# Second attention layer: score tiles of 64 columns, blockwise fetches, maxima turned by a 4-byte transfer, a longer lead

## The chip, the core and the metric

The kernel runs on one core of a Trainium2 chip, as one program launch. The metric is device time in microseconds (us), the median over several executions. Beside it stands one execution taken by the hardware profiler, from which every row below comes. Engines: PE is the matrix engine, PEld its weight loads, DVE the vector engine, ACT the scalar engine, POOL GpSimd, SP the engine whose queue issues nearly all of the DMA transfers here.

## What is computed

Two layers follow one another, on `x` of 2 x 2048 tokens and 256 features, in f32. Each computes attention on a layer norm, times a gate from another network, and adds that to `x`. Only the attention of the second layer is touched. It has 16 heads of 16 features and a band: a query sees the keys at most 64 tokens away.

```python
band = jnp.abs(idx[:, None] - idx[None, :]) <= WINDOW // 2      # WINDOW = 128
...
scores = jnp.einsum('bhqd,bhkd->bhqk', q, k) * SCALE + mask
attn = jax.nn.softmax(scores, axis=-1)
out = jnp.einsum('bhqk,bhkd->bhqd', attn, v)
...
x = x + s * g
```

## The kernel before

One function, `attention`, serves both layers; `local` is true for the second. Its work is cut into 32 **items**, one for each batch row `b` (2), group `g` of four heads (4) and block `n` of 512 queries (4). In the second layer an item has two **units** of two query tiles of 128 each (`U = 2`), 64 units in all. The four heads of a group lie on the partitions 0 to 31, 32 to 63 and so on of the tiles `q` and `k`, so each head's matmul uses 32 rows of PE's array.

Each unit is worked on in two passes. The **first pass** finds each query's greatest score: `sq` is a score tile with queries on the 128 output partitions and a reach of 256 keys in the free dimension (192 at the two ends of the sequence). DVE adds the band's mask to it and takes the maximum in one instruction (`seen`, result in `mx`, L674). The **second pass** computes the scores again with keys on the partitions (`sk`), with the query's maximum already subtracted: row `HD` of each head's 32 rows of `q` carries the negative maximum, against a row of ones in `k`. ACT takes the exponential out of PSUM (L683), POOL zeroes what lies outside the band (four `affine_select` per unit, L688), and two units later PE multiplies by the values (`acc`, L747, with the softmax's sum in an extra column). ACT copies the sum out to `av` (L752).

`scores` issues the matmuls of both passes for one step. Before they are issued they are sorted by a number, `when`, so that matmuls of different heads alternate and their tiles run beside each other. The first pass runs ahead of the second: at step `s` the second pass is at unit `s`, the first at unit `s + U + LEAD`. `LEAD` is 3 in the second layer, so the first pass is five units ahead.

Maxima come to where they are needed in `place_max` (from L714): PE transposes `mx` into PSUM (`pmx`, L720), ACT copies it negated to `row` (L723), and ACT's own queue issues a transfer of `row` into `q` (L726). The first layer does it in another way, with `turn_max` and `fetch_max` (L700 to L712): DVE negates into `nmx`, SP writes it to DRAM in turned order (`md`), and three units later SP fetches it back into `q`.

Division by the softmax's sum takes a round trip through DRAM, all by SP, in program order: `av` to `ad` (L773), the sums back as `dn` and the numerators to `xn` (L782, L783), DVE's reciprocal (L786), `dn` to `rd` (L789), and `rd` spread to `recb` (L796). Then `divide` multiplies, by turns on POOL and on DVE (L802). After the last group of a block, `project` multiplies by the output weights (L835) and updates `x`.

`fetch` brings `k` and `q` of a head group from DRAM (`qd`) by SP, in halves of the sequence, into one of two pairs of tiles. The dictionary `after` names the step after which each of these helpers is called. What is wrapped in `pin` keeps its program order on its engine; the rest is ordered by the framework. SP executes its queue in order, so a transfer that waits holds up those behind it.

Of the kernel before, what the change touches and what calls it, by code (L numbers as in the profile page):

```python
# [10 lines left out]
F32 = mybir.dt.float32  # L11
I32 = mybir.dt.int32
AF = mybir.ActivationFunctionType
ALU = mybir.AluOpType
# [3 lines left out]
P = 128  # L18
# [19 lines left out]
def two_layers(ctx: ExitStack, tc: tile.TileContext, a, out):  # L38
# [445 lines left out]
    def attention(A, scale, local, final, start=None, projected=False):  # L484
# [15 lines left out]
        U = TT // 2 if local else NT  # L500
        LEAD = 3 if local else 6
        DEL = 2 if local else 1
        with ExitStack() as st:
# [44 lines left out]
            mp, op = pool("mp", 2), pool("op", 1)  # L548
            hp = [slice(j * HP, (j + 1) * HP) for j in range(NG)]
            ep = None if local else pool("ep", 8)  # L550


            pmax, pm = pool("pmax", 2, space=PSUM), pool("pexp", 4, space=PSUM)
            if local:

                mask = mp.tile([P, 2 * P], F32, name="mask", bufs=1)
                nc.vector.memset(mask, 0.0)
                nc.gpsimd.affine_select(
                    out=mask, in_=mask, compare_op=ALU.is_ge, fill=MASKED, base=0,
                    pattern=[[1, 2 * P]], channel_multiplier=-1,  # L560
                )
                nc.gpsimd.affine_select(
                    out=mask, in_=mask, compare_op=ALU.is_ge, fill=MASKED, base=P,
                    pattern=[[-1, 2 * P]], channel_multiplier=1,
                )

                efirst = xn[1].rearrange("p c t -> p (c t)").rearrange("p (i s c f) -> p i s c f", i=4, c=2, f=P)
                elast = op.tile([P, 2, 4, 2, P], F32, name="elast")
                ecount = [0]

                def exponentials():

                    r = ecount[0] % 6
                    ecount[0] += 1
                    return efirst[:, r] if r < 4 else elast[:, r - 4]
# [4 lines left out]

            def fetch(bg, lo=0, hi=T):

                if bg >= B * NG:
                    return
                b, g = divmod(bg, NG)
                k0, k1 = max(lo - PAD, 0), (T if hi == T else hi - PAD)
                for i, t in ((1, qs[bg % 2]), (0, ks[bg % 2])):
                    to, s = (slice(lo, hi), slice(lo, hi)) if i else (slice(PAD + k0, PAD + k1), slice(k0, k1))
                    nc.sync.dma_start(out=t[:, to], in_=qd[i, b, bass.ts(g, NG), :, s].rearrange("h w t -> (h w) t"))
# [6 lines left out]
            def scores(second, first, es):  # L596
# [7 lines left out]
                if second:  # L604
# [3 lines left out]
                    if local:  # L608

                        qt = n * TT + 2 * u  # L610
                        segs = [
                            (P, 3 * P, bass.ts(qt + 1, P), bass.ds(qt * P, 2 * P)),
                            (0, P, bass.ts(qt, P), bass.ts(qt, P)),
                            (3 * P, 4 * P, bass.ts(qt + 2, P), bass.ts(qt + 1, P)),
                        ]
                    else:
                        segs = [(0, TB, bass.ts(u, P), bass.ts(n, TB))]
                    if local:
# [7 lines left out]
                    for j in range(NG):  # L626
# [4 lines left out]
                        else:  # L631
                            t = pm.tile([P, TB], F32, name="sk", tag="m")
                        when = 2 * (j // 2) if apart else 0
                        for lo, hi, ks_, qs_ in segs:
                            pieces.append((when, t[:, lo:hi], k[hp[j], ks_], q[hp[j], qs_]))
                            when += 2 * (hi - lo) / TB
                        tasks.append((es[j], t))
                pairs = []
                if first:
# [9 lines left out]
                    for pair in ((2, 3), (0, 1)):  # L649
                        sq = pmax.tile([P, 2, TB], F32, name="sq", tag="sq")  # L650
                        pairs.append((pair, sq))
                        for d, j in enumerate(pair):
                            when = (2, 2, 0, 0)[j] if apart else 0
                            if local:
                                for t in range(2):
                                    qt, lo, hi = reach(n1, u1, t)
                                    pieces.append((
                                        when + t, sq[:, d, t * 2 * P + lo : t * 2 * P + hi],
                                        q1[hp[j], bass.ts(qt, P)], k1[hp[j], qt * P + lo : qt * P + hi],
                                    ))  # L660
                            else:
# [6 lines left out]
                for pair, sq in pairs:  # L668
                    if local:
                        for d, j in enumerate(pair):  # L670
                            for t in range(2):
                                qt, lo, hi = reach(n1, u1, t)
                                seen = mp.tile([P, 2 * P], F32, name="seen", tag="seen")
                                nc.vector.tensor_tensor_reduce(  # L674
                                    seen[:, lo:hi], sq[:, d, t * 2 * P + lo : t * 2 * P + hi], mask[:, lo:hi],
                                    1.0, LOWEST, ALU.add, ALU.max, mx[:, j, 2 * u1 + t : 2 * u1 + t + 1],
                                )
# [14 lines left out]

            def reach(n, u, t):

                qt = n * TT + 2 * u + t
                return qt, (PAD if qt == 0 else 0), (2 * P - PAD if qt == NT - 1 else 2 * P)

            pin = tc.keep_in_program_order
# [8 lines left out]
            def fetch_max(i):  # L707
# [3 lines left out]
                    in_=md[i % 2].rearrange("(j t) p -> j (t p)", t=TT),  # L711
                ))  # L712

            def place_max(i):  # L714

                b, g, n = items[i]
                q = tiles(i)[0]
                mx, _ = part.pop(i)
                ps = pm.tile([NG * TT, P], F32, name="pmx", tag="m")
                nc.tensor.transpose(ps, mx.rearrange("p j t -> p (j t)"), ident)  # L720
                row = mp.tile([NG * TT, P], F32, name="row", tag="row", bufs=2 if local else 1)
                if local:
                    pin(nc.scalar.activation(row, ps, AF.Copy, scale=-1.0))  # L723
                else:
                    nc.vector.tensor_scalar(row, ps, -1.0, None, ALU.mult)
                pin((nc.scalar if local else nc.sync).dma_start(  # L726
                    out=q[HD:P:HP, bass.ts(n, TB)].rearrange("j (t c) -> j t c", c=P), in_=row
                ))
# [69 lines left out]
            def divide(i):  # L798

                b, g, n = items[i]  # L800
                pin(
                    (nc.vector if local and i % 2 else nc.gpsimd).tensor_tensor(together(b, g, n), together(b, g, n), divs.pop(i), ALU.mult)  # L802
                )
# [55 lines left out]
            for i, (b, g, n) in enumerate(items):  # L859
                if local:  # L860
                    at(i * U - LEAD, place_max, i)
                else:
                    at(i * U - LEAD, turn_max, i)
                    at(i * U - LEAD + 3, fetch_max, i)
                end = (i + 1) * U
# [324 lines left out]
```

## Time and profile before

| | us |
|---|---|
| median of three runs | 2537.28 |
| their range | 2533.64 to 2539.33 |
| the profiled execution | 2538.34 |
| its span | 2536.6 |

The second layer's attention begins at 2248 us of the span and fills the rest of it. Busy time of the engines there, by stretches, from the windows view:

| stretch, us | what runs | PE | DVE | ACT | POOL |
|---|---|---|---|---|---|
| 2248 to 2303 | last projections of keys, queries and values, first pass ahead, then both begin | 53.9 | 24.3 | 25.6 | 7.9 |
| 2303 to 2405 | both passes | 101.3 | 92.8 | 75.5 | 84.9 |
| 2405 to 2453 | both passes with output projections | 47.9 | 36.9 | 25.7 | 39.7 |
| 2453 to 2496 | both passes | 41.7 | 39.0 | 31.0 | 36.4 |
| 2496 to 2537 | second pass alone, last projections | 35.6 | 19.0 | 16.7 | 24.6 |

How such rows are read: a line of a group begins with the kernel's line number and the engine, then the operation, the tile written, an arrow and the tiles read, and the shape. For PE, `32*128 32x256` is a tile of 32 rows and 128 columns of the array, through which 256 columns of moving data stream. A product of f32 matrices is two such instructions in the trace. PE counts as busy while any matmul is in flight, so a busy PE need not be at its peak.

### The profile page before, as it was taken

The numbers are of one execution on the slowest core, as the hardware profiler recorded it, in microseconds if no ns is written. First come the engines' busy times: TensorE is split into PE (matmuls) and PEld (weight loads), VectorE is DVE, ScalarE is ACT, GpSimd is POOL, SyncE is SP. The second block draws the span as 40 slices with busy tenths as digits, with TensorE's granted clock in tenths as the row PEclk, the third lists the DMA queues.
The fourth block names the chain that finished last, engine by engine and source line by source line (L and its number), as shares of the span: only waits on it lengthen the run. The fifth ranks groups of instructions, "written<-read, shape, count | busy, mean of one in ns | idle before, by whom it ended". The sixth has DMA issues, their size and how long they took to land.

```text
span 2536.6 us, 47898 instructions
## 1 busy us (share of the span) xinstructions
PE 2513.1 (99%) x18896; PEld 1060.6 (42%) x18896; DVE 1686.2 (66%) x2747; ACT 1620.8 (64%) x3187; POOL 876.6 (35%) x827
## 2 busy tenths in 40 slices
PE   8999999999999999999999999999999999999999
PEld 6444444444333333333333333333333334457766
DVE  4143333157888888888777788788888765238986
ACT  5400000126888888888888888888888886227755
POOL 0000000102444444444444444444444420016887
PEclk9999999999999999999999999999999999999999
DMA  6131111230001001001001001001000002133552
GB/s 243 50 84 51 52 51 39 82 118 14 14 14 43 16 12 44 16 12 44 16 12 43 10 18 44 12 17 43 15 14 10 14 14 63 49 133 108 163 167 81
DMA packets 146353, 129.83 MB, mean 51 GB/s; under 512 B 93456, under 2 KB 97936, under 8 KB 143568
## 3 DMA queue, kind: packets, MB, share of 16 engines
q1 hardware_dynamic: 144256, 125.46, 16.5%
q8 instruction: 148, 2.42, 0.4%
q10 hardware_dynamic: 1872, 1.31, 0.2%
q14 instruction: 77, 0.63, 0.1%
HBM read 80.50 MB, written 45.97 MB: 50 GB/s over the span
## 4 chain that ended last, share of the span: by engine, by line
PE 79%; DMA 1%; ACT 0%; POOL 0%; DVE 0%; issue 0%; ACTq 0%; SPq 0%; POOLq 0%; DVEq 0%
PE sk L667 25%; PE acc L747 22%; PE sq L667 19%; PE pp L477 5%; PE pr L835 2%; PE pp L532 2%; PE po L1027 1%; PE pt L1023 1%; PE po L1035 1%; PE xb L113 0%; PE xb L138 0%; DMA k<-qd 0%; PE of L827 0%; DMA q<-qd 0%; POOL xn L688 0%
## 5 line engine op out<-in xcount | busy, mean ns | idle before, releaser
L679 DVE TENSOR_REDUCE part<-sq 128x2 f32<-128x1024 f32 x1024 | 1207.3, 1221 | 294.3 <-PE sq L667 284.7
L683 ACT ACTIVATE e<-sk 128x512 f32<-128x512 f32 x2048 | 1058.3, 603 | 217.2 <-PE sq L667 197.7
L667 PE MATMUL sk<-q,k 32*128 32x512 f32 (+2 forms) x5632 | 1135.8, 533 | 1.2 <-ACT xn L683 1.0
L667 PE MATMUL sq<-k,q 32*128 32x512 f32 (+2 forms) x5120 | 1129.1, 569 | 0.5 <-DVE part L679 0.5
L761 POOL TENSOR_TENSOR av<-av,more 128x512 f32<-128x512 f32 x459 | 581.4, 1267 | 936.3 <-ACT more L760 931.1
L667 PEld LDWEIGHTS sk<-q,k 32*128 32x128 f32 x5632 | 522.0, 184 | 604.1 <-ACT e L683 512.5
L747 PE MATMUL acc<-e,v 128*32 128x512 f32 x4096 | 546.7, 605 | 0.0
L667 PEld LDWEIGHTS sq<-k,q 32*128 32x128 f32 x5120 | 402.3, 183 | 22.3 <-DVE part L679 13.2
L760 ACT COPY more<-acc 128x512 f32<-128x512 f32 x459 | 268.7, 585 | 1.2 <-PE acc L747 1.0
L747 PEld LDWEIGHTS acc<-e,v 128*32 128x32 f32 x4096 | 81.8, 108 | 388.2 <-ACT e L683 367.8
L461 ACT ACTIVATE gt<-po 128x512 f32<-128x512 f32 x16 | 8.8, 594 | 321.1 <-PE po L457 321.1
L674 DVE CUSTOM_DVE_ANT_0 seen<-sq,mask 128x256 f32<-128x256 f32 (+1 forms) x512 | 176.2, 410 | 53.6 <-PE sq L667 49.2
L467 POOL TENSOR_TENSOR x<-x,up 128x512 f32<-128x512 f32 x16 | 23.1, 1461 | 450.1 <-DVE up L464 277.5
L448 DVE TENSOR_TENSOR xs<-we,px 128x512 f32<-128x512 f32 x64 | 43.9, 686 | 136.2 <-PE px L440 130.3
L688 POOL TENSOR_SCALAR_AFFINE_SELECT xn<-xn 128x512 f32<-128x512 f32 x172 | 106.2, 652 | 77.4 <-ACT xn L683 75.7
L440 PE MATMUL px<-xn,FV 128*128 128x512 f32 x256 | 121.2, 595 | 0.0
L444 PE MATMUL py<-cum,FW 128*128 128x512 f32 x256 | 120.5, 593 | 0.6 <-DVE cum L412 0.6
L424 PE MATMUL po<-pr,UO 128*128 128x512 f32 x256 | 119.0, 592 | 0.0
L683 ACT ACTIVATE xn<-sk 128x512 f32<-128x512 f32 x172 | 89.8, 602 | 41.1 <-PE sk L667 17.9
L450 DVE TENSOR_TENSOR pr<-xs,py 128x512 f32<-128x512 f32 x64 | 44.0, 687 | 64.8 <-PE py L444 64.6
L424 PEld LDWEIGHTS po<-pr,UO 128*128 128x128 f32 x256 | 48.6, 190 | 61.2 <-issue 61.0
L444 PEld LDWEIGHTS py<-cum,FW 128*128 128x128 f32 x256 | 48.4, 190 | 61.5 <-issue 59.8
(195 smaller groups left out, 1604.0 us busy)
## 6 DMA issues: line engine op xcount, KB each, us to landing
we<-wd SPq DMA_DIRECT2D x128, 128.0 KB
ad<-av SPq DMA_DIRECT2D x59, 256.0 KB
qd<-sb SPq DMA_DIRECT2D x48, 256.0 KB
k<-qd SPq DMA_DIRECT2D x10, 1024.0 KB
q<-qd SPq DMA_DIRECT2D x10, 1024.0 KB
xn<-ad SPq DMA_DIRECT2D x59, 128.0 KB
recb<-rd SPq DMA_DIRECT2D x59, 128.0 KB
q<-qd SPq DMA_DIRECT2D x12, 512.0 KB
```

Source lines behind the costliest of these rows:

```text
L424: nc.tensor.matmul(po[oc], UO[:, ch, bass.ts(oc, P)], pr, start=(ch == 0), stop=False)
L440: nc.tensor.matmul(px, FV[:, c, bass.ts(ch, P)], xn[b][:, c, cols], start=(c == 0), stop=(c == NC - 1))
L444: nc.tensor.matmul(py, FW[:, c, bass.ts(ch, P)], cum[:, c, :], start=(c == 0), stop=(c == NC - 1))
L477: nc.tensor.matmul(ps, w[:, c, bass.ts(hf, P)], xn[b][:, c, bass.ts(n, TB)], start=(c == 0), stop=(c == NC - 1))
L667: nc.tensor.matmul(o, lhs, rhs, start=True, stop=True)
L674: nc.vector.tensor_tensor_reduce(seen[:, lo:hi], sq[:, d, t * 2 * P + lo : t * 2 * P + hi], mask[:, lo:hi], 1.0, LOWEST, ALU.add, ALU.max, ...
L679: nc.vector.tensor_reduce(pt[:, pair[0] : pair[1] + 1, t, kb], sq, AX.X, ALU.max)
L683: nc.scalar.activation(e, t, AF.Exp, scale=scale)
L688: nc.gpsimd.affine_select(out=e[:, :, c, :], in_=e[:, :, c, :], compare_op=ALU.is_ge, fill=0.0, base=0, pattern=[[0, 4], [sign, P]], chann ...
L747: nc.tensor.matmul(acc[hp[j], o : o + hi - lo], vs[b][:, kt, vcols(g, j)], es[j][:, lo:hi], start=(r == 0), stop=(r == len(parts) - 1), sk ...
L760: nc.scalar.copy(more, acc)
L761: nc.gpsimd.tensor_tensor(avs[i], avs[i], more, ALU.add)
```

## The change

Six edits, all to the second layer:

- First pass: a tile of 128 queries becomes two halves of 64, each with its own window of 192 keys. The two halves write partitions 0 to 63 and 64 to 127 of the same PSUM tile. The mask is built once in three forms (inside, first tile, last tile).
- Second pass: each block of 128 keys is split into two halves of 64 too, with the same moving data. The matmuls of both passes now use tiles of 32 rows and 64 columns.
- Maxima go the way of the first layer, `turn_max` and `fetch_max`; `place_max` is removed.
- The first pass runs eight units ahead (`LEAD` 6).
- `k` and `q` are fetched by blocks of 512 tokens, after every item, `k` one unit before `q`.
- `divide` goes to DVE in three of four items, not in two of four.

```diff
-        LEAD = 3 if local else 6
+        LEAD = 6
...
+            halves = [slice(sub * P // 2, (sub + 1) * P // 2) for sub in range(2)]
+            RC = P + 2 * PAD // 2
...
+                mask = mp.tile([P, 3, RC], F32, name="mask", bufs=1)
+                for m in range(3):
+                    for sub, p in enumerate(halves):
+                        nc.vector.tensor_copy(mask[p, m, :], reach[p, sub * PAD : sub * PAD + RC])
+                nc.vector.memset(mask[halves[0], 1, :PAD], MASKED)
+                nc.vector.memset(mask[halves[1], 2, RC - PAD :], MASKED)
...
-            def fetch(bg, lo=0, hi=T):
+            def fetch(bg, lo=0, hi=T, which=(1, 0)):
...
                         segs = [
-                            (P, 3 * P, bass.ts(qt + 1, P), bass.ds(qt * P, 2 * P)),
-                            (0, P, bass.ts(qt, P), bass.ts(qt, P)),
-                            (3 * P, 4 * P, bass.ts(qt + 2, P), bass.ts(qt + 1, P)),
+                            (sub, lo, hi, bass.ds((qt + kt) * P + sub * PAD, PAD), bass.ds(q0, hi - lo))
+                            for kt, lo, hi, q0 in (
+                                (1, P, 3 * P, qt * P), (0, 0, P, qt * P), (2, 3 * P, 4 * P, (qt + 1) * P)
+                            )
+                            for sub in range(2)
                         ]
...
-                        when = 2 * (j // 2) if apart else 0
-                        for lo, hi, ks_, qs_ in segs:
-                            pieces.append((when, t[:, lo:hi], k[hp[j], ks_], q[hp[j], qs_]))
-                            when += 2 * (hi - lo) / TB
+                        when = [1.5 * (j // 2) if apart and local else 2 * (j // 2) if apart else 0] * 2
+                        for sub, lo, hi, ks_, qs_ in segs:
+                            o = t[:, lo:hi] if sub is None else t[halves[sub], lo:hi]
+                            pieces.append((when[sub or 0], o, k[hp[j], ks_], q[hp[j], qs_]))
+                            when[sub or 0] += 2 * (hi - lo) / TB
...
                                 for t in range(2):
-                                    qt, lo, hi = reach(n1, u1, t)
-                                    pieces.append((
-                                        when + t, sq[:, d, t * 2 * P + lo : t * 2 * P + hi],
-                                        q1[hp[j], bass.ts(qt, P)], k1[hp[j], qt * P + lo : qt * P + hi],
-                                    ))
+                                    for sub in range(2):
+                                        q0 = (n1 * TT + 2 * u1 + t) * P + sub * PAD
+                                        pieces.append((
+                                            when + t * RC / (2 * P), sq[halves[sub], d, bass.ts(t, RC)],
+                                            q1[hp[j], bass.ds(q0, PAD)], k1[hp[j], bass.ds(q0, RC)],
+                                        ))
...
-                                seen = mp.tile([P, 2 * P], F32, name="seen", tag="seen")
+                                seen = mp.tile([P, RC], F32, name="seen", tag="seen")
                                 nc.vector.tensor_tensor_reduce(
-                                    seen[:, lo:hi], sq[:, d, t * 2 * P + lo : t * 2 * P + hi], mask[:, lo:hi],
+                                    seen, sq[:, d, bass.ts(t, RC)], mask[:, (qt == 0) + 2 * (qt == NT - 1), :],
                                     1.0, LOWEST, ALU.add, ALU.max, mx[:, j, 2 * u1 + t : 2 * u1 + t + 1],
                                 )
...
-            def place_max(i):
...
-                    (nc.vector if local and i % 2 else nc.gpsimd).tensor_tensor(together(b, g, n), together(b, g, n), divs.pop(i), ALU.mult)
+                    (nc.vector if local and i % 4 else nc.gpsimd).tensor_tensor(together(b, g, n), together(b, g, n), divs.pop(i), ALU.mult)
...
-                if local:
-                    at(i * U - LEAD, place_max, i)
-                else:
-                    at(i * U - LEAD, turn_max, i)
-                    at(i * U - LEAD + 3, fetch_max, i)
+                at(i * U - LEAD, turn_max, i)
+                at(i * U - LEAD + 3, fetch_max, i)
...
-                if local and n == NB // 2 - 1:
-                    at(end, fetch, b * NG + g + 2, 0, T // 2)
-                if n == NB - 1:
-                    at(end, fetch, b * NG + g + 2, T // 2 if local else 0)
+                if local:
+
+                    for hop, which in enumerate((0, 1)):
+                        at(end + hop, fetch, b * NG + g + 2, n * TB, (n + 1) * TB, (which,))
+                elif n == NB - 1:
+                    at(end, fetch, b * NG + g + 2)
```

More of the change, by code (lines that the diff above doesn't have):

```diff
@@ L554, in attention @@
             if local:
-                mask = mp.tile([P, 2 * P], F32, name="mask", bufs=1)
-                nc.vector.memset(mask, 0.0)
+                reach = mp.tile([P, 2 * P], F32, name="reach", bufs=1)
+                nc.vector.memset(reach, 0.0)
                 nc.gpsimd.affine_select(
-                    out=mask, in_=mask, compare_op=ALU.is_ge, fill=MASKED, base=0,
+                    out=reach, in_=reach, compare_op=ALU.is_ge, fill=MASKED, base=0,
                     pattern=[[1, 2 * P]], channel_multiplier=-1,
@@ L562, in attention @@
                 nc.gpsimd.affine_select(
-                    out=mask, in_=mask, compare_op=ALU.is_ge, fill=MASKED, base=P,
+                    out=reach, in_=reach, compare_op=ALU.is_ge, fill=MASKED, base=P,
                     pattern=[[-1, 2 * P]], channel_multiplier=1,
                 )
+                mask = mp.tile([P, 3, RC], F32, name="mask", bufs=1)
[4 more added lines that the diff above has]
+                nc.vector.memset(mask[halves[1], 2, RC - PAD :], MASKED)
                 efirst = xn[1].rearrange("p c t -> p (c t)").rearrange("p (i s c f) -> p i s c f", i=4, c=2, f=P)
@@ L586, in fetch @@
                 k0, k1 = max(lo - PAD, 0), (T if hi == T else hi - PAD)
-                for i, t in ((1, qs[bg % 2]), (0, ks[bg % 2])):
+                for i in which:
+                    t = (ks, qs)[i][bg % 2]
                     to, s = (slice(lo, hi), slice(lo, hi)) if i else (slice(PAD + k0, PAD + k1), slice(k0, k1))
@@ L611, in scores @@
                         segs = [
-                            (P, 3 * P, bass.ts(qt + 1, P), bass.ds(qt * P, 2 * P)),
-                            (0, P, bass.ts(qt, P), bass.ts(qt, P)),
-                            (3 * P, 4 * P, bass.ts(qt + 2, P), bass.ts(qt + 1, P)),
+                            (sub, lo, hi, bass.ds((qt + kt) * P + sub * PAD, PAD), bass.ds(q0, hi - lo))
[3 more added lines that the diff above has]
+                            for sub in range(2)
                         ]
                     else:
-                        segs = [(0, TB, bass.ts(u, P), bass.ts(n, TB))]
+                        segs = [(None, 0, TB, bass.ts(u, P), bass.ts(n, TB))]
                     if local:
@@ L671, in scores @@
                             for t in range(2):
-                                qt, lo, hi = reach(n1, u1, t)
-                                seen = mp.tile([P, 2 * P], F32, name="seen", tag="seen")
+                                qt = n1 * TT + 2 * u1 + t
+                                seen = mp.tile([P, RC], F32, name="seen", tag="seen")
                                 nc.vector.tensor_tensor_reduce(
-                                    seen[:, lo:hi], sq[:, d, t * 2 * P + lo : t * 2 * P + hi], mask[:, lo:hi],
+                                    seen, sq[:, d, bass.ts(t, RC)], mask[:, (qt == 0) + 2 * (qt == NT - 1), :],
                                     1.0, LOWEST, ALU.add, ALU.max, mx[:, j, 2 * u1 + t : 2 * u1 + t + 1],
@@ L691, in scores @@
                             )
-            def reach(n, u, t):
-                qt = n * TT + 2 * u + t
-                return qt, (PAD if qt == 0 else 0), (2 * P - PAD if qt == NT - 1 else 2 * P)
             pin = tc.keep_in_program_order
@@ L711, in fetch_max @@
                     in_=md[i % 2].rearrange("(j t) p -> j (t p)", t=TT),
-                ))
-            def place_max(i):
[L716 to L721, printed above, removed]
-                if local:
-                    pin(nc.scalar.activation(row, ps, AF.Copy, scale=-1.0))
-                else:
-                    nc.vector.tensor_scalar(row, ps, -1.0, None, ALU.mult)
-                pin((nc.scalar if local else nc.sync).dma_start(
-                    out=q[HD:P:HP, bass.ts(n, TB)].rearrange("j (t c) -> j t c", c=P), in_=row
                 ))
@@ L859, in attention @@
             for i, (b, g, n) in enumerate(items):
-                if local:
-                    at(i * U - LEAD, place_max, i)
-                else:
-                    at(i * U - LEAD, turn_max, i)
-                    at(i * U - LEAD + 3, fetch_max, i)
+                at(i * U - LEAD, turn_max, i)
+                at(i * U - LEAD + 3, fetch_max, i)
                 end = (i + 1) * U
```

## Prediction

> **What bounds the kernel now.** I read the page's chain first, to see whether one engine carries the end.
>
> ```profile
> PE 79%; DMA 1%; ACT 0%; POOL 0%; DVE 0%; issue 0%; ACTq 0%; SPq 0%; POOLq 0%; DVEq 0%
> ```
>
> Nearly all that is named is PE. The change touches layer two's attention alone, which fills the span from 2248 us on, so an average over the span says little. The windows view gives 102 us of its steady stretch, before any output projection:
>
> ```profile
> core 0: us, PE busy (x) PEld busy (x) DVE busy (x) ACT busy (x) POOL busy (x), PEclk, DMA share, GB/s
> 2303.00:2405.00 102.00, 101.30 (x2022) 81.21 (x2023) 92.79 (x519) 75.45 (x173) 84.92 (x132) 1.00 0.53 162
> ```
>
> DVE at 91% and POOL at 83% stand close behind PE. PE's own limit is seen in the timeline of one unit, matmuls (PE) and weight loads (PEld), start and length in us:
>
> ```profile
> 2345.19 0.48 PE L667 MATMUL sk<-q,k 32*128 32x256 f32 x2
> ...
> 2345.20 0.48 PE L667 MATMUL sq<-k,q 32*128 32x256 f32 x2
> 2345.29 0.19 PEld L667 LDWEIGHTS sk<-q,k 32*128 32x128 f32 x2
> ...
> 2345.51 0.38 PE L667 MATMUL sk<-q,k 32*128 32x256 f32 x2
> ...
> 2347.30 1.08 PE L747 MATMUL acc<-xn,v 128*32 128x128 f32 x24
> ...
> 2348.31 0.28 PE L720 MATMUL pmx<-ident,mx 128*16 128x128 f32 x1
> ...
> 2348.51 0.48 PE L667 MATMUL sk<-q,k 32*128 32x256 f32 x1
> ```
>
> Four matmuls, one per head's 32 rows, start together, and the next round follows about 0.216 us later per 256 columns (0.32 at a refill). So a unit is 2.11 us of scores, 1.01 us of acc, and in every second unit 0.20 us of pmx. The starts of acc in the trace lie 3.12 and 3.39 us apart in turn, with hardly an outlier: an item (two units) costs 6.51 us and **PE sets it**.
>
> **The change part by part, for one item.**
>
> *Half tiles on PE.* A score tile is now 32 rows by 64 columns, so eight fit. Per head and unit a tile streams 512 columns for sk and two times 192 for sq, against 512 and 512. A column costs 0.216/256 = 0.844 ns, and each product is two instructions: (512+384) x 2 x 0.844 = 1.51 us, against 1.73. The other 0.38 us of the 2.11 are two refills of 0.105 (a 128-column load takes 0.185; a 16-column load 0.088 and a 32-column one 0.109, so about 0.13 for 64), a 0.07 wait and the drain. I take 0.27. Score phase 1.78, unit 1.78 + 1.01 = 2.79. This rests on eight tiles running beside each other, which no row shows: rows show four by rows (above) and four by columns (acc). Ends: 1.51 us (all eight) and 3.02 us (two halves of a row group take turns). I take the first, because acc already runs several column tiles over the same rows.
>
> [...] the loads at 2345.29 run under the matmuls of the same heads, begun at 2345.19, and the acc group's 24 loads run under its own matmuls. By the row the loads cost nothing more, and I keep 2.79. [...]
>
> *The transpose goes.* pmx (0.20 on PE), its copy row (0.26 on ACT) and ACT's transfer issue (0.55) leave each item. PE per item: 2 x 2.79 = **5.58** instead of 6.51.
>
> *Maxima on DVE.* The edge tiles show the new form already:
>
> ```profile
> 2249.48 0.42 DVE L674 CUSTOM_DVE_ANT_0 seen<-sq,mask 128x256 f32<-128x256 f32 x1
> 2249.83 0.08 DVE L674 DVE_READ_ACCUMULATOR2_ANT mx<- 128x1 f32 x1
> 2249.83 0.35 DVE L674 CUSTOM_DVE_ANT_0 seen<-sq,mask 128x192 f32<-128x192 f32 x1
> 2250.10 0.08 DVE L674 DVE_READ_ACCUMULATOR2_ANT mx<- 128x1 f32 x1
> ```
>
> Start to start it is 0.345 for 256 columns and 0.275 for 192. Sixteen per item: 5.5 becomes 4.4. Added: nmx 0.17 (layer one's row), a quarter more of the divides (825 ns each on DVE, 0.21). With the reciprocal 0.25, DVE goes from 6.16 to **5.44**. The divide waits for recb; behind it in DVE's queue stand the next maxima, and the score matmuls wait for their PSUM.
>
> *POOL and ACT.* POOL: eight selects 4.9 plus a quarter of 1.27: 5.2 (was 5.5). ACT: eight exponentials 4.12 plus two copies 0.80: 4.9 (was 5.7). Neither is the bound.
>
> *Transfers of 4-byte elements.* Layer one does this. Its trace, an issue at 1722.89, by the microsecond:
>
> ```profile
> 1723.00:1724.00 1.00, 1.00 (x12) 0.26 (x7) 0.65 (x1) 0.75 (x2) 0.99 (x1) 1.00 0.10 1
> 1724.00:1725.00 1.00, 1.00 (x12) 0.16 (x8) 1.00 (x2) 1.00 (x3) 0.27 (x1) 1.00 0.75 7
> 1725.00:1726.00 1.00, 1.00 (x15) 0.65 (x15) 0.71 (x1) 0.80 (x2) 0.06 (x1) 1.00 0.08 1
> ```
>
> 2064 packets are through about 2.3 us after the issue began. [...] By the row it is 0.93 us of all engines' time (the three shares), 16% of a 5.8 us item atop 53% now: dear, but three units lie between write and fetch, so I cost its latency at nothing. If that cover is gone, ACT's exponentials and PE wait.
>
> *SP's queue.* This is where the change pays. Issues per item now: ad 0.54, dn 0.54, xn 0.60, rd 0.58, recb 0.53, and a k/q pair (0.82) in every second item: 3.2 us. After: the same five, a pair every item (0.82), md 0.38, q<-md 0.53: 4.52, plus nine gaps of 0.06 = 5.06 us. SP also waits in order; its waits in the 102 us (total, times, longest):
>
> ```profile
> SPq L796 <- DMA rd<-dn: 26.7, 13, 4.2
> SPq L782 <- DMA ad<-av: 9.8, 6, 4.3
> ```
>
> That is 2.05 us per recb, worst behind big fetches:
>
> ```profile
> 2357.27 0.53 SPq L589 DMA_DIRECT2D k<-qd  x1
> 2357.89 0.38 SPq L589 DMA_DIRECT2D q<-qd  x1
> 2358.32 0.58 SPq L789 DMA_DIRECT2D rd<-dn  x1
> 2358.95 1.37 SPq L773 DMA_DIRECT2D ad<-av  x1
> 2363.58 0.53 SPq L796 DMA_DIRECT2D recb<-rd  x1
> ```
>
> The fastest rd-to-recb is 1.95 us (2323.41 to 2325.36), of which rd, ad, md and their gaps will cover 1.6. So the wait is 0.3 at best and 1.5 or more behind a 256 KB pair (half the former size, but in every item). Cycle 5.4 to 6.6 or more; I take **5.95**, nearer the middle since smaller fetches spread the load. So behind PE, SP is late next.
>
> *Eight units ahead, fetch by block.* A fetched block has five or six units before its first use instead of seven; at 2.8 us that is 14 us or more against a landing of 2 to 5, hidden. Three more units run maxima alone at the start (about 0.9 us of PE each, under the last projections), three more run scores alone at the end (2.5 instead of 2.8, set by POOL and ACT). Shorter maxima in the other five give 1.2 back: +0.5 in sum, unsure by 3. The mask's six extra copies fall where DVE idles 8 us before 2249: nothing.
>
> *Sum.* Of 28 items with both passes, 20 have fetches and no projection: 20 x (6.51 - 5.95) = 11.2. Four have projections (units of 4.9 to 5.1, PE's) and four no fetch left; both follow PE's 5.58, with 0.07 for jitter: 8 x (6.51 - 5.65) = 6.9. Together 18.1, less 0.5 for the ends, less 0.2 per fetched item for divides that wait in DVE's queue (4): **about -13.5 us**. Against the profiled execution's own 2538.3 us (span 2536.6) this gives 2524.8; the three runs shown have the median 2537.3, 1.0 lower, so I say **2524**.
>
> **Rivals.**
> - *SP becomes the bound and loses* (slower). Place: recb, waiting behind rd in SP's queue, with a fetch pair ahead in every item; dn, q<-md and the DVE divide follow late. If each item pays the 2.05 us measured per recb plus a little on ad, a cycle is 7.3 us: 20 x 0.8 = +16, less 6.8 elsewhere, gives 2546. It decides from a cycle over 6.85, where 20 x 0.34 eats the 6.8 that the other items gain. For: SP has 4.5 us of issues where it had 3.2. Against: md and the fetches fill part of what was waiting, and the projections' 10 us items let SP catch up.
> - *Half tiles take turns*: score phase 3.3, unit 4.3, +1.18 x 56 = +66, 2603. For: no row shows eight. Against: both four-way rows.
> - *No full gain*: DVE, POOL and SP all within 10% of PE trade waits, an item near 6.4: 2534.
> - *Pure PE bound*: every plain item at 5.6, 24 x 0.91 + 3.4 = 25, 2512.
>
> **How the numbers follow.** 0.2%, 5.1 us here, is about what a measurement of this kernel can tell from no change. Forecast and pure PE bound together (2510 to 2532) 0.61; no full gain 0.14, mostly within 0.2%; SP's loss 0.17; tiles in turn 0.08. That makes faster 0.62, same 0.13, slower 0.25. The range, 2511 to 2547, leaves out the serial tiles and the worst of SP; the forecast's own is 2511 to 2532.
>
> **What would show it.** Eight starts within some 0.05 us and acc every 2.8 to 3.0 us would prove the tiles; rounds of four would refute them. The maxima should step by 0.275. No idle before sk or acc may end in a transfer. If SP's wait on rd stays near 2 us and the divides on DVE start late, SP is the bound and I am wrong about the sign.

## The result, and the profile after

| | us |
|---|---|
| before, median | 2537.5 |
| after, median of four runs | 2739.8 (2737.9 to 2746.5) |
| after / before | 1.0804, 95% interval 1.0782 to 1.0826 |
| span of the profiled execution after | 2744.8 |

The change costs about 202 us, and all of it lies in the second layer's attention. The page's chain of the kernel after, by engine, answers the one shown of before:

```profile
PE 72%; DMA 7%; issue 2%; DVE 1%; SPq 0%; ACT 0%; POOL 0%; ACTq 0%; DVEq 0%; POOLq 0%
```

DMA went from 1% to 7% of the span, and 7% is about 190 us. The windows view of the same 102 us:

```profile
core 0: us, PE busy (x) PEld busy (x) DVE busy (x) ACT busy (x) POOL busy (x), PEclk, DMA share, GB/s
2303.00:2405.00 102.00, 79.05 (x1794) 57.13 (x1796) 44.35 (x288) 43.17 (x87) 44.18 (x71) 0.78 0.51 68
```

No engine is at its limit: DVE, at 92.8 us before, is at 44.4, PE idles for 23 us, and its clock was 0.78 of full. The DMA engines are as busy as before (0.51 against 0.53) and move 68 GB/s instead of 162. SP's waits in this window (total, times, longest, us):

```profile
SPq L777 <- DMA ad<-av: 21.7, 4, 8.1
SPq L720 <- DMA md<-nmx: 18.7, 4, 9.4
SPq L791 <- DMA rd<-dn: 14.2, 4, 5.5
SPq L716 <- DMA q<-md: 8.4, 1, 8.4
```

They make 63 us of 102; before, `rd` and `ad` made 36.5. The timeline of one cycle of SP's queue, start and length:

```profile
2405.62 0.59 SPq L768 DMA_DIRECT2D ad<-av  x1
2406.31 0.38 SPq L716 DMA_DIRECT2D md<-nmx  x1
2411.29 0.54 SPq L791 DMA_DIRECT2D recb<-rd  x1
2414.16 0.53 SPq L777 DMA_DIRECT2D dn<-ad  x1
...
2417.34 0.54 SPq L720 DMA_DIRECT2D q<-md  x1
2417.93 0.58 SPq L784 DMA_DIRECT2D rd<-dn  x1
2418.55 1.13 SPq L768 DMA_DIRECT2D ad<-av  x1
```

From `ad` to `ad` it is 12.9 us, where the kernel before has 6.7 (mean) and the prediction 5.95. `q<-md` follows the write of `md` after 11.0 us, and `dn` follows the write of `ad` after 8.5. The chain of waits then runs nearly through DMA alone (start, length; the dots stand for 1.8 us, nearly all of it DVE's):

```profile
2417.93 4.70 DMA rd<-dn
2422.69 7.87 DMA recb<-rd
...
2432.34 11.65 DMA md<-nmx
```

The row that should have warned was there before. In layer one the write of `md` was issued at 1722.89 and SP's next instruction, `q<-md`, at 1733.40: 10.5 us, where the packets had ended 2.3 us after the issue. The landing events that the trace has of this write's semaphore come 8.4 to 10.4 us after the issue, so SP was waiting for the landing. One item of layer one lasts 46.8 us (from one `md` to the next), so it cost nothing there.

### The profile page after: what moved, and what is told of

The parts are those of the page before. It is cut to its first block, busy times and chain, and to the rows that moved or that the text cites. A ratio compares the mean times of both kernels' runs of the same rounds, so it can differ in the third digit from the quotient of the medians.

```text
span 2744.8 us, 53185 instructions
## 1 busy us (share of the span) xinstructions
PE 2616.3 (95%) x21424; PEld 1102.8 (40%) x21424; DVE 1666.1 (61%) x2794; ACT 1624.3 (59%) x3155; POOL 868.8 (32%) x820
## 4 chain that ended last, share of the span: by engine, by line
PE 72%; DMA 7%; issue 2%; DVE 1%; SPq 0%; ACT 0%; POOL 0%; ACTq 0%; DVEq 0%; POOLq 0%
PE sk L683 23%; PE acc L742 20%; PE sq L683 18%; PE pp L477 4%; PE pp L532 2%; PE pr L830 2%; DMA ad<-av 2%; DMA recb<-rd 2%; DMA md<-nmx 1%; PE po L1021 1%; DMA rd<-dn 1%; DMA dn<-ad 1%; PE pt L1017 1%; PE po L1029 1%; DMA q<-md 1%
## 5 line engine op out<-in xcount | busy, mean ns | idle before, releaser
L683 PE MATMUL sk<-q,k 32*128 32x512 f32 (+2 forms) x7168 | 1197.7, 519 | 38.9 <-issue 27.2
L683 PE MATMUL sq<-k,q 32*128 32x512 f32 (+1 forms) x6144 | 1156.1, 548 | 35.9 <-DVE mx L690 20.1
L683 PEld LDWEIGHTS sk<-q,k 32*128 32x128 f32 (+1 forms) x7168 | 538.2, 176 | 668.4 <-ACT e L699 514.7
L683 PEld LDWEIGHTS sq<-k,q 32*128 32x128 f32 (+1 forms) x6144 | 405.2, 176 | 74.0 <-issue 31.6
L690 DVE CUSTOM_DVE_ANT_0 seen<-sq,mask 128x192 f32<-128x192 f32 x512 | 148.8, 351 | 119.9 <-PE sq L683 71.2
L699 ACT ACTIVATE elast<-sk 128x512 f32<-128x512 f32 x84 | 45.4, 596 | 91.5 <-PE sk L683 39.9
L742 PE MATMUL acc<-xn,v 128*32 128x128 f32 (+1 forms) x1032 | 72.5, 384 | 23.7 <-issue 22.7
```

What stands on the lines that cost most here:

```text
L683: nc.tensor.matmul(o, lhs, rhs, start=True, stop=True)
L690: nc.vector.tensor_tensor_reduce(seen, sq[:, d, bass.ts(t, RC)], mask[:, (qt == 0) + 2 * (qt == NT - 1), :], 1.0, LOWEST, ALU.add, ALU.max ...
L699: nc.scalar.activation(e, t, AF.Exp, scale=scale)
L742: nc.tensor.matmul(acc[hp[j], o : o + hi - lo], vs[b][:, kt, vcols(g, j)], es[j][:, lo:hi], start=(r == 0), stop=(r == len(parts) - 1), sk ...
```

## The experiments

All ratios are to the kernel before, with a 95% interval. Matmul counts "a unit" in the expectations (128, 160, 176, 208) count weight loads too. SP's cycle (mean from `ad` to `ad`) and the time from `ad`'s issue to `dn`'s (median) are worked out from SP's rows between 2303 and 2405.

| kernel | us | ratio | SP's cycle | ad to dn |
|---|---|---|---|---|
| before | 2537.5 | | 6.7 | 4.3 |
| after | 2739.8 | 1.0804 (1.0782 to 1.0826) | 13.1 | 9.3 |
| after, maxima on PE again | 2562.1 | 1.0094 (1.0074 to 1.0114) | 8.3 | 4.7 |
| before, maxima by transfers | 2732.4 | 1.0774 (1.0758 to 1.0790) | 13.4 | 8.2 |
| after, small elements on the read | 2667.1 | 1.0517 (1.0499 to 1.0535) | 12.9 | 3.5 |
| after, fetch two steps later | 2749.0 | 1.0833 (1.0817 to 1.0849) | | |
| unread write, 2048 elements | 2728.9 | 1.0752 (1.0731 to 1.0772) | 13.3 | 10.1 |
| unread write, 1024 | 2714.5 | 1.0717 (1.0672 to 1.0762) | 13.9 | 8.1 |
| unread write, 512 | 2703.4 | 1.0656 (1.0625 to 1.0687) | 13.0 | 7.9 |
| unread write, 2048, 64 B apart | 2588.1 | 1.0204 (1.0183 to 1.0224) | 8.7 | 4.9 |
| unread write, 128 rows of 64 B | 2558.7 | 1.0086 (1.0058 to 1.0114) | 8.1 | 4.4 |

### Which part costs the 200 us

The changed kernel with `place_max` back in the second layer, all else of the change kept:

```diff
-                at(i * U - LEAD, turn_max, i)
-                at(i * U - LEAD + 3, fetch_max, i)
+                if local:
+                    at(i * U - LEAD, place_max, i)
+                else:
+                    at(i * U - LEAD, turn_max, i)
+                    at(i * U - LEAD + 3, fetch_max, i)
```

> The changed kernel with one part undone: the maxima are turned by PE again (place_max, ACT's queue), half tiles, lead of eight units, fetches by block and the divides stay. Theory A (the 4-byte write to DRAM lands about 10 us after its issue, and everything behind it in SP's order and behind its bytes waits): the loss goes, 2510 to 2535 us. Theory B (eight half tiles, or the longer stream of PE instructions, are slow by themselves): stays within 30 us of 2740. Theory C (fetches by block overload SP): falls only in part, to 2600 to 2700.

The kernel before with the maxima's way alone (and the lead that it needs):

```diff
-        LEAD = 3 if local else 6
+        LEAD = 6
...
-                if local:
-                    at(i * U - LEAD, place_max, i)
-                else:
-                    at(i * U - LEAD, turn_max, i)
-                    at(i * U - LEAD + 3, fetch_max, i)
+                at(i * U - LEAD, turn_max, i)
+                at(i * U - LEAD + 3, fetch_max, i)
```

> The kernel before with the maxima alone changed: turned by the 4-byte write and fetched back by SP, with the lead of eight units that this needs; full tiles, fetches by halves. Theory A: most of the loss appears, 2660 to 2760 us, and SP waits some 2 us or more per item for md and for ad. Theory B: 2530 to 2550, since the tiles are the old ones. Theory C: 2540 to 2600.

2562 and 2732: from either side the transfer of the maxima is 178 to 195 us (the 195 hold the longer lead too, 7 us alone as shown below). The rest of the change, 24 us slower, is no gain either.

### Waiting for the landing, or standing behind it

The changed kernel, writing `md` as 128 rows of 64 B and turning on the read:

```diff
-                pin(nc.sync.dma_start(out=md[i % 2].rearrange("j p -> p j"), in_=nmx))
+                if local:
+                    pin(nc.sync.dma_start(out=mr[i % 2], in_=nmx))
...
+                        in_=mr[i % 2].rearrange("p (j t) -> j t p", t=TT),
```

> The changed kernel, but the maxima are written to DRAM in 128 rows of 64 bytes, and the 4-byte elements are on the side of the read that brings them into q. Same bytes, same two SP transfers, same waits. If under theory A it is the small writes into DRAM that land late: 2515 to 2580 us. If any transfer of 2048 elements of 4 bytes lands as late: 2700 to 2760. Theory B: about 2740.

2667, between the two. `ad` now lands early (3.5 us to `dn`, the median), but the chain of this run shows the small elements late on the side of `q`:

```profile
2333.12 7.83 DMA q<-mr
...
2353.17 9.06 DMA q<-mr
```

And SP itself is held up: its next issue behind each `q<-mr` takes 5.4 us (median of 16 between 2303 and 2495; 4.5 to 6.7), where an issue otherwise takes about 0.55. This loss has another path than that of the write, and turning on the read is no cure: it costs 105 us more than PE's transpose (2562).

The maxima turned by PE again (2562 by itself), with the negated maxima written to DRAM besides, where nobody reads them:

```diff
+                if local:
+                    nmx = mp.tile([P, NG * TT], F32, name="nmx", tag="nmx", bufs=8)
+                    pin(nc.vector.tensor_scalar(nmx, mx.rearrange("p j t -> p (j t)"), -1.0, None, ALU.mult))
+                    pin(nc.sync.dma_start(out=md[i % 8].rearrange("j p -> p j"), in_=nmx))
```

> The first experiment's kernel (transpose on PE restored), which besides writes each item's negated maxima to DRAM by SP in turned order, 2048 elements of 4 bytes, eight buffers in turn. Nobody reads them, so nothing waits for their landing; the output is the reference's. Theory A (the cost is SP's wait for the write's landing, before the fetch of the maxima): only an issue of 0.38 us and a gap per item is added, 2558 to 2582 us. Theory B (a backlog: behind the small elements every other transfer of SP's lands late, whoever reads them): well above, 2610 to 2745.

The changed kernel, fetching later:

```diff
-                at(i * U - LEAD + 3, fetch_max, i)
+                at(i * U - (1 if local else LEAD - 3), fetch_max, i)
```

> The changed kernel with the maxima's fetch two steps later in the second layer (one step ahead of its use, five behind the write, at 2.8 us or more each 14 us against a landing after 10.4), and four md buffers for two. Theory A (SP's wait for the landing, in order, holds up the division's transfers): the wait finds the write landed, 2555 to 2620 us. Theory B (backlog behind the small elements): the other transfers stay late, 2690 to 2750.

2729 and 2749. My first theory, that SP waits for the landing and so holds up the rest, fell: with no reader the write costs 167 us more than the kernel without it, and a later fetch regains nothing.

### Number of elements, or their place

The unread write with half and with a quarter of its elements (here half; 4 for 8 in the quarter):

```diff
-                    pin(nc.sync.dma_start(out=md[i % 8].rearrange("j p -> p j"), in_=nmx))
+                    pin(nc.sync.dma_start(out=md[i % 8][:8].rearrange("j p -> p j"), in_=nmx[:, :8]))
```

> The unread write with half of its elements, 1024 of 4 bytes per item. Theory A (each 4-byte element occupies its DMA engine for some 80 ns, 10.4 us times 16 engines over 2048, and SP's cycle is the elements' time plus about 2.2 to 3 us of the other transfers): elements 5.2 us, cycle 7.4 to 8.3 against 6.6 without, 2580 to 2620 us. Theory B (a fixed delay for a write of small elements, whatever their number): 2700 to 2745.

> The unread write with a quarter of its elements, 512 per item. Theory A (time per element): 2.6 us of elements, cycle 4.8 to 5.6, under what PE needs: 2560 to 2580 us. Theory B (fixed delay): 2700 to 2745.

A time per element fell as well: a quarter still costs 141 of the 167 us. The windows view of the quarter shows a cycle, microsecond by microsecond (columns as above); `ad` was issued at 2361.92, `md` at 2362.91:

```profile
2363.00:2364.00 1.00, 1.00 (x53) 1.00 (x59) 0.13 (x1) 0.31 (x2) 1.00 (x2) 1.00 0.91 278
2364.00:2365.00 1.00, 0.94 (x49) 0.73 (x38) 1.00 (x9) 0.95 (x2) 0.20 (x1) 1.00 0.31 43
2365.00:2366.00 1.00, 1.00 (x32) 0.68 (x32) 1.00 (x9) 1.00 (x3) 0.73 (x2) 1.00 0.13 18
2366.00:2367.00 1.00, 0.70 (x29) 0.42 (x19) 0.34 (x3) 0.12 (x1) 1.00 (x2) 1.00 0.00 0
2367.00:2368.00 1.00, 0.00 (x0) 0.00 (x0) 0.00 (x0) 0.00 (x0) 1.00 (x2) 1.00 0.00 0
```

By 2366 the packets are through (shares 0.13, 0.00, 0.00), DMA is silent and PE runs dry. What is waited for is in the trace's landing events of `ad`'s semaphore, sixteen for each write of `ad`:

```
2363.96 2363.96 2363.98 2364.01 2364.01 2364.05 2364.08 2364.08
2364.16 2364.28 2364.30 2364.37 2364.42 2364.49 2371.14 2371.18
```

Fourteen events come within 2.6 us of `ad`'s issue, the other two 6.7 us later, and SP issues `dn` at 2371.19. The events on record for `md`, issued after `ad`, come at 2370.77 to 2371.56, beside the late two. This is no single case: between 2303 and 2495 of the kernel after, ten writes of `ad` have all sixteen events on record, and in each of them one to three events come over 6 us after the issue; of the 23 in the control with rows (below) none has such an event. So `ad` (large packets) lands late where small elements lying side by side are issued after it, and nobody has to read `md` for it to cost. By what way, no run shows.

What remains is why the write is slow whatever the number of its elements. With fewer rows of `md` the elements still lie side by side in each row. So, all 2048 again, but 64 B apart:

```diff
+            mw = [dr.tile([NG * TT, P, 16], F32, name=f"mw{i}", tag=f"mw{i}") for i in range(8 if local else 0)]
...
-                    pin(nc.sync.dma_start(out=md[i % 8].rearrange("j p -> p j"), in_=nmx))
+                    pin(nc.sync.dma_start(out=mw[i % 8][:, :, 0].rearrange("j p -> p j"), in_=nmx))
```

> The unread write of all 2048 elements, but with the elements 64 B apart in DRAM instead of side by side. Theory A [...]: the landing comes early and the loss goes, 2558 to 2620 us. Theory B (the delay belongs to any write of 4-byte elements, wherever they fall): 2695 to 2745.

And as a control the same instruction at the same place, with contiguous rows:

```diff
-                    pin(nc.sync.dma_start(out=md[i % 8].rearrange("j p -> p j"), in_=nmx))
+                    pin(nc.sync.dma_start(out=mr[i % 8], in_=nmx))
```

> The unread write as 128 rows of 64 B, not turned: the same 8 KB by the same instruction at the same place in SP's queue, behind the same DVE negation. Theory A (small elements are what lands late): only an issue of 0.4 us per item is added, 2558 to 2582 us. Theory C (SP's in-order wait for DVE's negated maxima, ahead of the division's transfers, is the cost, whatever is written): 2690 to 2745.

2588 and 2559. The control is as fast as the kernel without the write (2562), so neither SP's extra issue nor its wait for DVE is the cost. Elements 64 B apart cost 29 us more than rows; side by side they cost 170. So it is neither the number of elements nor their size alone, but **4-byte writes next to one another in DRAM**. Why, no run shows: the elements 64 B apart also spread over 128 KB instead of 8, no distance between 4 and 64 B was tried, and no trace shows the memory's side.

### Half tiles

| kernel | us | ratio |
|---|---|---|
| before, half tiles in both passes | 2554.8 | 1.0071 (1.0051 to 1.0091) |
| before, half tiles in the first pass | 2779.7 | 1.0954 (1.0937 to 1.0970) |
| before, half tiles in the second pass | 2930.7 | 1.1556 (1.1537 to 1.1575) |
| first pass, sorted by tile size | 2576.3 | 1.0161 (1.0140 to 1.0181) |
| before, full tiles, more instructions | 2549.0 | 1.0045 (1.0028 to 1.0063) |

The kernel before with the change's tiles, mask and `seen` alone (its `LEAD`, fetches, maxima and divides stay), in the core of it:

```diff
+                            for sub in range(2)
...
+                            o = t[:, lo:hi] if sub is None else t[halves[sub], lo:hi]
+                            pieces.append((when[sub or 0], o, k[hp[j], ks_], q[hp[j], qs_]))
...
+                                            when + t * RC / (2 * P), sq[halves[sub], d, bass.ts(t, RC)],
+                                            q1[hp[j], bass.ds(q0, PAD)], k1[hp[j], bass.ds(q0, RC)],
```

> The kernel before with half tiles in both passes alone; lead of five units, fetches by halves, place_max and the divides as before. Theory A: PE's score phase falls from 2.1 us towards 1.8 and acc comes every 2.8 to 3.0 us, 2512 to 2532 us. Theory B: 2650 or more.

Slower by 18 us, outside the range of either theory. The timeline of PE in this run, two units (in brackets idle time before, and what ended it):

```profile
2344.48 0.45 PE L683 MATMUL sk<-q,k 32*64 32x256 f32 x4
2344.51 0.56 PE L683 MATMUL sq<-k,q 32*64 32x192 f32 x8
...
2346.42 1.08 PE L758 MATMUL acc<-elast,v 128*32 128x128 f32 x24
2347.43 0.65 PE L683 MATMUL sk<-q,k 32*64 32x256 f32 x7
2349.13 0.42 PE L683 MATMUL sk<-q,k 32*64 32x256 f32 x1 [1.05 <-issue]
```

In the first unit eight tiles start within 0.05 us; the scores take 1.94 us (2.11 before, 1.78 predicted) and the whole 2.95 (3.12 and 2.79). It is no exception: 49 units lie between 2303 and 2495, and in the 12 without idle time the scores take 1.95 us (median). So half of the predicted gain of a unit is there. In the second unit PE stops after seven matmuls of a group of eight, for nothing recorded ("issue"). A packet of 16,384 B of the queue that the page calls `q8 instruction` landed at 2347.66; PE went on 1.47 us later. In the stretch from 2303 to 2495 this kernel has 13 idle times of PE over 0.3 us, 15.6 us in sum; 11 of them (12.7 us) end 1.2 to 1.6 us after such a packet landed, though the packets come 4.7 us apart, which by chance would put one in twelve there. Before, there is one idle time, 0.64 us after a packet. So, as far as times can tell, PE's instructions came too late. From the layer's first maximum to the end PE is busy 277.2 us (279.3 before) and idle 28.4 us (8.1 before): the idle time is the whole loss. The page counts 168 packets on that queue for 148 before: 20 x 16,384 B for 64 units of 80 instructions more. An estimate from these counts: 64 B each, so a packet is 256 instructions, two units before and 1.23 units with half tiles. If that is so, more instructions must bring such idle time without any half tile:

> The kernel before, full tiles, each product of 256 moving columns cut into two of 128: 176 matmuls a unit for 128, the same columns streamed, tile sizes unchanged. Theory A (PE outruns its instruction supply at such a density): idle of PE that ends 1.2 to 1.6 us after an instruction packet has landed, several us of it between 2303 and 2495, 2542 to 2575 us. Theory B (the idle in the half-tile kernel has to do with the half tiles): no such idle, 2533 to 2542, or slower with PE busy throughout if twice the loads do not hide.

That kernel splits 256 moving columns into two of 128 in both passes, tiles unchanged:

```diff
-                            (P, 3 * P, bass.ts(qt + 1, P), bass.ds(qt * P, 2 * P)),
+                            (P, 2 * P, bass.ts(qt + 1, P), bass.ts(qt, P)),
+                            (2 * P, 3 * P, bass.ts(qt + 1, P), bass.ts(qt + 1, P)),
...
+                                    for c0, c1 in ((lo, P), (P, hi)):
```

2549, with 7 idle times over 0.3 us, five of them in the same band after a packet (not the longest, 3.1 us). Its page counts 12 packets more than before, which at the estimated 64 B are the 48 instructions a unit that it has more. Such idle time comes with the instructions, then, and needs no half tiles.

Fewer instructions, then: half tiles in the first pass alone save the same columns with 160 instructions. Its edit takes the kernel with both and gives the second pass its full tiles back. The counterpart has half tiles in the second pass alone:

```diff
-                            (sub, lo, hi, bass.ds((qt + kt) * P + sub * PAD, PAD), bass.ds(q0, hi - lo))
-                            for kt, lo, hi, q0 in (
-                                (1, P, 3 * P, qt * P), (0, 0, P, qt * P), (2, 3 * P, 4 * P, (qt + 1) * P)
-                            )
-                            for sub in range(2)
+                            (None, P, 3 * P, bass.ts(qt + 1, P), bass.ds(qt * P, 2 * P)),
+                            (None, 0, P, bass.ts(qt, P), bass.ts(qt, P)),
+                            (None, 3 * P, 4 * P, bass.ts(qt + 2, P), bass.ts(qt + 1, P)),
```

> The kernel before with half tiles in the first pass alone (second pass in tiles of 128 columns as before): PE issues 160 matmuls a unit, against 128 before and 208 with half tiles in both; the columns streamed are the same as with both. Theory A (the gain of 0.22 us a unit is real, and half tiles in both passes lost it since PE's instructions arrive too slowly for 208 a unit): gaps of PE rare, 2512 to 2534 us. Theory B (tiles of 64 columns themselves stall or take turns beside others): 2545 to 2570. In between, near 2537: the gain is eaten by fewer gaps, or by tiles of 64 and of 128 columns that do not run beside each other.

> The kernel before with half tiles in the second pass alone: 176 matmuls a unit, no column less to stream. Theory A (PE's instruction supply is what half tiles cost): slower, 2542 to 2562 us, with idle of PE that nothing recorded explains and that ends a fixed time after an instruction packet has landed. Theory B (the loss of both-pass half tiles comes from the first pass): no change, 2533 to 2541.

Both were far off. The windows view, the first pass's kernel and then the second's:

```profile
2303.00:2405.00 102.00, 102.00 (x917) 55.46 (x921) 28.60 (x189) 29.87 (x63) 29.32 (x47) 0.50 0.18 56
```

```profile
2303.00:2405.00 102.00, 102.00 (x869) 44.54 (x869) 28.74 (x163) 26.19 (x55) 25.58 (x41) 0.50 0.15 48
```

PE is never idle, yet its clock is half. The scores of one unit in the first-pass kernel's timeline (PE):

```profile
2342.96 1.22 PE L681 MATMUL sk<-q,k 32*128 32x256 f32 x4
2344.11 1.56 PE L681 MATMUL sq<-k,q 32*64 32x192 f32 x16
2345.60 1.25 PE L681 MATMUL sk<-q,k 32*128 32x128 f32 x12
2346.78 0.92 PE L681 MATMUL sq<-k,q 32*64 32x192 f32 x8
2347.63 0.80 PE L681 MATMUL sk<-q,k 32*128 32x128 f32 x4
2348.36 0.92 PE L681 MATMUL sq<-k,q 32*64 32x192 f32 x8
2349.20 0.80 PE L681 MATMUL sk<-q,k 32*128 32x128 f32 x4
```

Tiles of 64 and of 128 columns are in groups that follow one another: each group starts as the one before ends. The size changes six times in these seven groups; in the second-pass kernel it changes eight times a unit. Sorted so that nearly all `sq` come before all `sk` (two changes a unit):

```diff
-                        when = [1.5 * (j // 2) if apart and local else 2 * (j // 2) if apart else 0] * 2
+                        when = [10 if apart and local else 2 * (j // 2) if apart else 0] * 2
...
-                            when = (2, 2, 0, 0)[j] if apart else 0
+                            when = (2, 2, 0, 0)[j] if apart and not local else 0
```

> The kernel with half tiles in the first pass alone, with the matmuls of a unit sorted otherwise: first all of the first pass (tiles of 64 columns), then all of the second (128 columns), so that the tile size changes twice a unit rather than six times. Theory A (tiles of the two sizes do not run beside each other[...]): most of the loss goes, clock over 0.9, 2545 to 2660 us; ACT gets its four tiles at once, so a gain on the kernel before is not expected. Theory B (two sizes in a unit cost the clock, however they are sorted): clock near 0.5 in the stretch, over 2740.

```profile
2303.00:2405.00 102.00, 93.88 (x2101) 63.86 (x2102) 66.40 (x434) 61.98 (x143) 70.47 (x110) 1.00 0.44 135
```

2576, clock 1.00. With two, six and eight changes a unit the clock in the stretch is 1.00, 0.50 and 0.50 and the time 2576, 2780 and 2931 us (the last with the halves in the other pass). Between the first two only the sort differs: the alternation of sizes cost the clock. How, no run shows.

### The edits that were costed at nothing

| kernel | us | ratio |
|---|---|---|
| lead, blocks and divides together | 2555.0 | 1.0077 (1.0052 to 1.0103) |
| lead alone | 2543.6 | 1.0026 (1.0018 to 1.0033) |
| fetches by blocks alone | 2550.1 | 1.0056 (1.0039 to 1.0072) |
| divides alone | 2541.6 | 1.0020 (1.0010 to 1.0029) |

Each is the change's own edit, put into the kernel before: the lead, the fetches, the divides.

```diff
-        LEAD = 3 if local else 6
+        LEAD = 6
...
+                    for hop, which in enumerate((0, 1)):
+                        at(end + hop, fetch, b * NG + g + 2, n * TB, (n + 1) * TB, (which,))
...
-                    (nc.vector if local and i % 2 else nc.gpsimd).tensor_tensor(together(b, g, n), together(b, g, n), divs.pop(i), ALU.mult)
+                    (nc.vector if local and i % 4 else nc.gpsimd).tensor_tensor(together(b, g, n), together(b, g, n), divs.pop(i), ALU.mult)
```

> The kernel before with the remaining edits alone: first pass eight units ahead, k and q fetched by blocks of 512 tokens, the divide on DVE in three of four items; full tiles, maxima on PE as before. Theory A (these edits are hidden, as predicted): 2533 to 2541 us. Theory B (they are what separates the first and the fourth experiment, more units at the ends or more transfers at a time): 2541 to 2550.

> The kernel before with the first pass eight units ahead, that edit alone. Theory A (the lead costs its three units of maxima alone at the start, less what the end gives back): 2536 to 2543 us; the rest of the 22 us of the twelfth experiment is then the fetches by blocks and the divides. Theory B (the lead is most of it): 2550 to 2560.

> The kernel before with k and q fetched by blocks of 512 tokens after every item, that edit alone. Theory A (a fetch in every item puts SP's recb further behind, in every item instead of every fourth; most of the 15 us that the twelfth experiment cost beyond the lead): 2544 to 2556 us. Theory B (hidden, as predicted; the 15 us come from the lead and the blocks together or from the divides): 2533 to 2541.

> The kernel before with the divide on DVE in three of four items, that edit alone. Theory A (DVE, at 91% in the stretch, gets 0.21 us more per item while its divides wait for recb with maxima behind them): 2538 to 2548 us. Theory B (POOL's relief outweighs it or neither matters): 2530 to 2538.

By their ratios they cost about 7, 14 and 5 us alone, and 20 together. In the kernel with all three the second pass begins 4.3 us later than before (first `acc` at 2303.1 against 2298.8). For the blocks the trace does not settle the cause: SP's wait for `rd` in their own run (40.8 us between 2303 and 2495) is hardly above the 39.6 of before. Nor do the parts add up: half tiles (18) and these edits (20) make 38 alone, and 24 in one kernel.

No kernel tried beat the one before.

## Why the prediction was wrong

- **The step that failed** is the one on 4-byte elements: "2064 packets are through about 2.3 us after the issue began", and from it "I cost its latency at nothing". The packets' end is not the landing. The landing stood 10.5 us behind the issue, in a row of the trace of before, and read as SP's pacing. Even with 10.5 us for `md` itself the sum would have failed (a fetch two steps later regains nothing, 2749), because the price is paid by the other transfers: `ad` to `dn` from 4.3 to 9.3 us, SP's cycle from 6.7 to 13.1.
- **The price of the 4-byte elements** was weighed in engine time, 0.93 us an item. With elements 64 B apart the price is indeed small (29 us in 32 items); with elements side by side it is six times that, and the row chosen could not show it.
- **SP loses** was the rival with the right place (SP's transfers of the division) and sign. Its 2546 came from more issues and waits of the old length. The issues were sized well, the waits not.
- **Half tiles**: the tiles run side by side, with eight starts within 0.05 us and 2.95 us for a unit without idle. But the term was mis-sized: 2.79 were predicted, and the gain is 0.17 us a unit, not 0.33. Where the other 0.16 us go, no run shows. What was gained was then lost to idle times of PE that the sum did not have, 28.4 us for 8.1 (between 2303 and 2495, 12.7 of 15.6 us end 1.2 to 1.6 us behind an instruction packet): 18 us more in all.
- **Lead, blocks, divides**: the first two were put at +0.5 us and cost 7 and 14 alone; the divides were put at 4 us of waits and cost 5. The landing of 2 to 5 us was the author's estimate: between 2300 and 2495 the fetches of before land 3.7 to 6.7 us after their issue, still within the 14.
- **What would show it** named the right sign: an idle of SP on `rd` and late divides. Eight starts together and no transfer before `sk` were meant as two tests of one case; the first held and the second did not.

## What to carry to other kernels

Take the landing of a transfer from the next instruction that waits for it, not from its packets, and ask which other transfers land late beside it (`ad` to `dn`: 4.3 us before, 9.3 after). Avoid writes of single 4-byte elements that lie side by side in DRAM while other transfers matter: they cost 167 us here. The same bytes as rows of 64 B cost nothing (2559 us against 2562), but turning them on the read then held up SP's issues (5.4 us for 0.55). Before splitting matmuls, count instructions per microsecond as well as columns (80 more a unit came with 20.3 us more idle time of PE), and do not alternate tile sizes within a unit (clock 0.50 with six changes, 1.00 with two).

## What the runs showed of the hardware

- In layer one a write of 2048 elements of 4 bytes ended its packets in 2.3 us and landed after 10.4, on otherwise quiet DMA engines. In the second layer, with 512 such elements side by side written after it, `ad` had landed only 9.3 us after its issue.
- With half tiles PE resumed 1.2 to 1.6 us after a 16,384 B instruction packet had landed, in 11 of its 13 idle times over 0.3 us (2303 to 2495).
- Tiles of 32 rows by 64 and by 128 columns followed one another (a group starts within 0.1 us of the end of the one before), and with six changes a unit the clock stayed at 0.50 for over 100 us with PE busy throughout (1.00 with two changes).
- In the kernel after, the clock also fell behind an idle time of PE, and late. The windows view:

```profile
2417.00:2418.00 1.00, 0.00 (x0) 0.00 (x0) 0.00 (x0) 0.00 (x0) 0.00 (x1) 1.00 0.44 41
2418.00:2419.00 1.00, 0.00 (x0) 0.00 (x0) 0.48 (x4) 0.00 (x0) 1.00 (x1) 1.00 0.93 235
2419.00:2420.00 1.00, 0.10 (x8) 0.11 (x12) 1.00 (x8) 0.00 (x0) 0.93 (x3) 1.00 0.80 175
...
2421.00:2422.00 1.00, 1.00 (x32) 0.94 (x32) 1.00 (x8) 0.95 (x2) 1.00 (x3) 0.51 1.04 233
2422.00:2423.00 1.00, 1.00 (x24) 0.47 (x16) 0.64 (x5) 0.36 (x2) 1.00 (x3) 0.50 0.81 11
```

  PE is idle for 3.0 us (2416.92 to 2419.90), is busy again for one, and then runs at half clock (0.51, 0.50) beside full work. That stall is followed by a second loss, at the clock; what ties the two, no run shows. Over the 102 us the clock is 0.78.
